# Two attention blocks on one core: v by the seven-product scheme used twice, in one row with output, k and q, and group statistics on ScalarE

## The chip, the cores and the metric

The kernel runs on one core of a Trainium2 chip. The metric is the device time of one execution in microseconds (us). In the text TensorE is PE in the profile (its weight loads PEld), VectorE is DVE, ScalarE is ACT, GpSimd is POOL, and SP is the engine that issues most DMAs.

## The reference, cut to what matters

Two attention blocks follow each other on x of shape (8, 512, 32, 32), all float32. Both compute the same thing up to the order of the weights:

```python
xn  = group_norm(x, 8 groups over channels and pixels) * gamma + beta      # (B, C=512, S=1024)
q, k, v = (W[i] @ xn + b[i] for i in range(3))                             # 512 x 512 each
p   = softmax(q_h^T k_h / 8) for each of 8 heads of 64 channels            # 1024 x 1024
out = concat_h(p_h v_h)
x   = x + Wp @ out + bp
```

The second block takes the first block's x.

## The kernel before

**Jobs.** A job is one image in one block; there are 16. They are ordered in groups of four: two images in the first block, then the same two in the second. A job has a *row* of projections and an *attention*. The row of job n computes v of job n, then the output projection (O) of job n - 1, then k and q of job n. The attention of job n follows.

**Seven products.** A product of two matrices, each cut in 2 x 2 blocks, is formed from seven block products instead of eight. The sums of weight blocks are kept in seven slots (`A11, S3, A12, A22, S1, S2, S4`); sums of the other operand's blocks are made by `combine` (into `tx`, `to` and in place). `v_phase` uses the scheme once: 7 products, each for two groups of tokens, each of four matmuls with 256 moving columns; that is 56 matmuls. Its blocks are put together in two PSUM bank groups, a result copied by ScalarE or added by VectorE into v. `deep_phases` uses the scheme twice for O, k and q: each of the seven outer products is again a chain of seven matmuls of 128 x 128 x 256, 49 in all for each. The inner sums of the other operand come from `inner_sums` (tile `deep`, for k and q) or `OutputSums` (tiles `os`, for O). Chains overlap in pairs: product j of chain c stands at place 7c + 2j. Each chain takes four banks of one half of PSUM; halves alternate from chain to chain. Its first results go to a tile `p` from the pool `epool` (6 buffers, shared with the attention's e tiles), and VectorE adds these up (`outer`).

**Attention.** 64 steps: eight groups (four pairs of heads, two halves of the query pixels) of eight blocks of keys. In step i TensorE forms the scores (`scores`, 8 matmul instructions), ScalarE takes their exponential (`e`), VectorE adds e to `acc` for the row sums, and two steps later TensorE multiplies with v into `po` (`values`). After each group `finish` adds the two halves of `po` into q; after every second group the row sums are inverted and q is normalised. Work for the next job is put between the steps as `chores`: statistics, normalisation, `combine`, inner sums, and the first weight fetches.

**What sets the order.** TensorE, ScalarE and VectorE run each in the order in which the program was written out. Python code writes it, with a clock of its own (`clock`, `advance`, `later`) that says when a thing is appended. No scheduler moves anything on these three engines. SP issues DMAs in the order written; weights come through a ring of 7 tiles (`fetch`, `used`). PSUM is two halves; `banks` closes one pool and opens the next, and a tile that lies where an older one was waits for that one's last reader.

**Factors of the weights.** The first time that a weight factor of O, k or q is used, `prepare` makes its inner sums on VectorE (4 additions of 128 x 128) and stores the result in DRAM; later fetches bring the finished 448 KB. For v the fetched block of 256 KB is used as it is.

**Statistics.** For every job except 0 and 1 VectorE reads x with eight `bn_stats` of 128 x 512, as `extra` work from the row's sixteenth chain on and, what is left over, in the first steps of attention. Job 1's statistics are made by ScalarE in attention 0: four passes that sum x and four that sum squares, with the sums read out by `accum_out`.

**Lines that the steps touch** (of the kernel before): v's matmuls L494, its copies L518 and additions L520; the matmuls of O, k and q L636; chain copies L438 and L442, results L646 to L657; additions of `p` L668 and of x L684 and L682; inner sums L423 to L429; `combine` L385 to L391; accumulations of e L893 and L895; in `finish` the reduction L925, the copy px L931 and the addition q<-po,px L932.

Of the kernel before, what the change touches and what calls it, by code (L numbers as in the profile page):

```python
# [9 lines left out]
F32 = mybir.dt.float32  # L10
# [9 lines left out]
P = 128  # L20
# [26 lines left out]
RING = 7  # L47
BLOCK = {1: (0, 0), 2: (0, 1), 4: (1, 1)}


# [22 lines left out]
def fast_path(  # L73
# [99 lines left out]
    def fetch():  # L173


        if not plan or len(held) == RING:
            return
        key = plan.popleft()
        n, which, o = key
        layer = jobs[n][1]  # L180
        w = ring.tile([P, NW, P], F32, tag="w", name=f"w_{which}_{n}_{o}")
        held[key] = w
        if (which, layer, o) in deep:
            nc.sync.dma_start(w, deep[which, layer, o])
        else:
            if o in BLOCK:
                src = raw_block(layer, which, *BLOCK[o])
            else:
                src = factors[which, layer][:, FACTOR[o]]
            nc.sync.dma_start(wide(w), src)  # L190
            if which != V:
                raw.add(key)
# [162 lines left out]
    def norm_steps(n):  # L355
# [5 lines left out]
        def factors():  # L361
            norm.factors(slice(0, NC))
            if n > 1:
                place()

        if n == 1:
            reads = [place] + [lambda cc=cc: norm.sums(cc) for cc in range(NC)]
            reads.append(norm.less_mean)
            reads += [lambda cc=cc: norm.squares(cc) for cc in range(NC)]
            reads.append(lambda: (norm.by_count(), norm.gather()))  # L370
            return reads, [norm.groups, factors] + [lambda cc=cc: norm.apply(cc) for cc in range(NC)]
# [202 lines left out]
    def deep_phases(n, extra, outs=None, early=()):  # L574
# [4 lines left out]
        dst = {}  # L579
        chains = [(which, o) for which in ((O, K, Q) if outs else (K, Q)) for o in OUTER]  # L580
        tiles = {}

        def job(which):
            return n - 1 if which == O else n

        def begin(c):
            which, o = chains[c]
            m = job(which)
            b, layer = jobs[m]
            if o == OUTER[0] and which != O:  # L590
                name = "k" if which == K else "q"
                dst[which] = acts.tile([P, NC, S], F32, tag=name, name=f"{name}_{n}")
                (kt if which == K else qt)[0] = dst[which]
            if c + 2 < len(chains):
                ahead, oo = chains[c + 2]
                prepare((job(ahead), ahead, oo))
            if which == O and c in (3, 4):
                soon.extend(outs.steps(c + 2))
            e = epool.tile([P, 2, HALF], F32, tag="e", name=f"p_{n}_{c}")
            tiles[which, o] = e  # L600
            s5 = small.tile([P, QT], F32, tag="s5", name=f"s5_{n}_{c}", bufs=3)
            half = (c + len(chains)) % 2
# [3 lines left out]
            if which == O:  # L606
                r = right(outs.src, to[0], o)
                sums = outs.at[c]
            else:
# [24 lines left out]

            def product(i, ps, start):
                nc.tensor.matmul(  # L636
                    ps, lhs[:, FACTOR[i], :], moving[i], start=start, stop=True,
                    skip_group_check=True,
                )

            def put(oo, ph, ps):
                to_ = e[:, oo, ph * QT : (ph + 1) * QT]
                b = bias(oo)
# [15 lines left out]
        def end(c):  # L659
# [6 lines left out]

            def add(to_, a, b):
                outer.append(lambda: nc.vector.tensor_add(to_, a, b))  # L668

            if which == O:  # L670
# [3 lines left out]
                def more(oh, sh, part, moved=False):  # L674
# [5 lines left out]
                    def go():  # L680
                        if moved:
                            nc.gpsimd.dma_start(to_, p(part), accum_op=ALU.add)  # L682
                        else:
                            nc.vector.tensor_add(to_, to_, p(part))  # L684
                        parts[oh, sh] -= 1
                        waiting[oh, sh] -= 1
# [19 lines left out]
                elif o == 6:  # L706
                    add(p(6), p(6), p(1))
                    more(0, 1, 6)
# [3 lines left out]
                elif o == 7:  # L712
                    add(p(7), p(7), p(6))
                    more(1, 0, 7)
# [5 lines left out]
                return  # L720
            d = dst[which]

            def quarter(oh, sh):
                return d[:, 2 * oh : 2 * oh + 2, sh * HALF : (sh + 1) * HALF]

            if o == 2:
                add(quarter(0, 0), p(1), p(2))
            elif o == 6:
                add(p(6), p(6), p(1))
            elif o == 5:  # L730
                add(quarter(0, 1), p(6), p(5))
            elif o == 7:
                add(p(7), p(7), p(6))
                add(quarter(1, 1), p(7), p(5))
            elif o == 3:
                add(quarter(0, 1), quarter(0, 1), p(3))
            elif o == 4:
                add(quarter(1, 0), p(7), p(4))

# [4 lines left out]
        def thunk(c, j):  # L744
            def go():
                if j == 0:
                    live[c] = begin(c)
                order = LAST_ORDER if c + 1 == len(chains) else ORDER
                live[c](order[j])
                if order[j] in (7, 3):  # L750
                    if soon:
# [7 lines left out]
                if j == 6:  # L759
                    end(c)  # L760
                    if c + 1 == len(chains):
                        while outer:
                            outer.popleft()()
                advance(0.43)

# [9 lines left out]
        ]  # L775
        return [thunk(c, j) for c, j in at]

# [80 lines left out]
    class Attention:  # L858
# [132 lines left out]

        def run(self, chores):

# [7 lines left out]
            for i in range(3, len(steps) + LEAD):  # L1001
                if i < len(steps):
                    self.scores(i)
                self.values(i - LEAD)
                g, kc = steps[i - LEAD]
# [27 lines left out]

    def out_sums(n, outs):

        def start():
# [3 lines left out]
        def part(i):  # L1042
            return lambda: combine(outs.src, to[0], i)

        c0, c1, c2, c3, c4 = (outs.steps(c) for c in range(5))
        steps = c0 + [start] + c3 + c1 + [part(1)] + c2 + [part(2)] + c4 + [part(3)]
        times = (0.1, 1.0, 2.5, 4.5, 5.5, 6.5, 7.5, 8.6, 14.0, 15.8, 16.5, 17.5, 19.2, 21.0)
# [20 lines left out]
    def extend_plan(n):  # L1068
        plan.extend((n, V, o) for o in ORDER)
        plan.extend((n - 1, O, o) for o in ORDER)  # L1070
        plan.extend((n, which, o) for which in (K, Q) for o in OUTER)
# [212 lines left out]
    for n in range(-1, len(jobs)):  # L1284
        last = n + 1 == len(jobs)
        outs = None
        if n >= 0:
# [11 lines left out]
            else:  # L1299
# [9 lines left out]
                if n == 0:  # L1309
                    for i, fn in zip((3, 3, 4, 5, 6, 8, 10, 11, 12, 13, 15), reads):  # L1310
                        put(i, fn)
                    at = (22, 30, 34, 35, 37, 38, 41, 44, 47, 50)
                for i, fn in zip(at, steps + sums(n + 1)):
                    put(i, fn)
                deep_first = deep_steps(n + 1)
                for at, fn in zip((52, 54, 57, 59), deep_first[4:]):
                    put(at, fn)
                put(61, lambda: (extend_plan(n + 1), [fetch() for _ in range(RING)]))
            assert max(chores, default=0) < NT * len(att.groups)
            att.run(chores)  # L1320
            banks(0, "one")
# [21 lines left out]
            if n + 2 < len(jobs):  # L1343
                reads, steps = norm_steps(n + 2)
                extra.extend((15, fn) for fn in reads)
        both = deep_phases(n + 1, extra, outs, deep_first[:4] if outs else ())
        both[0]()
# [260 lines left out]
```

## Time and profile before

| | |
|---|---|
| Time, median of 3 runs | 3204.76 us (3204.22 to 3205.25) |
| Profiled execution: span, first to last instruction | 3202.4 us |
| Outside the span | 2.4 us, by the median (the profiled execution has its span alone) |
| TensorE busy in the span | 3183.5 us (99%) |
| VectorE, ScalarE, GpSimd busy | 2773.9, 1914.3, 99.5 us |
| Row of job 3, row of job 6 | 90.14, 87.83 us |
| Attention of job 6 | 110.03 us |
| Granted TensorE clock | 0.999 |

A row of the timeline has the start in us from the span's start, its length in us, engine, line, operation, tiles (out<-in), shapes, and the count of instructions merged; in brackets stands how long the engine was idle before and what ended that. Instructions are pipelined: the length shown of one is longer than the distance to the next. A float32 matmul is two instructions in the trace.

### The profile page before, as it was taken

Reading aid. Unit: us, or ns where it says so; the run is one execution under the profiler, and the core shown is the slowest. Engines: PE = TensorE matmul, PEld = TensorE weight load, DVE = VectorE, ACT = ScalarE, POOL = GpSimd, SP = SyncE. Lnnn points to the kernel's source line nnn. Section 1 sums busy time; section 2 is a strip of 40 time slices with the busy share of each in tenths; the row PEclk is TensorE's granted clock in tenths of the full one; section 3 lists DMA queues with packets and bytes.
Section 4 is the critical chain, followed back from the end, with each engine's and each line's share of the span. In section 5 each row is a group of like instructions: output and inputs, shape, how many; then the busy total and the mean of one; then the engine's idle time right before and its main releaser. Section 6 shows DMA issues by size and latency. Waiting matters only on the chain.

```text
span 3202.4 us, 57786 instructions
## 1 busy us (share of the span) xinstructions
PE 3183.5 (99%) x22917; PEld 1862.2 (58%) x22917; DVE 2773.9 (87%) x3990; ACT 1914.3 (60%) x3063; POOL 99.5 (3%) x94
## 2 busy tenths in 40 slices
PE   9999999999999999999999999999999999999999
PEld 7366384663836648366483754837547375573744
DVE  8897999979889798897988889888898888978878
ACT  4746646466565665656656565565656656566564
POOL 0000000000000000000000000000000000000000
PEclk9999999999999999999999999999999999999999
DMA  8234172350713315034170421504316051150611
GB/s 291 74 105 123 49 216 67 95 166 22 213 25 90 89 28 158 22 105 130 31 211 16 117 69 37 149 16 137 101 44 194 16 138 48 49 136 16 174 37 42
DMA packets 156726, 307.80 MB, mean 96 GB/s; under 512 B 34088, under 2 KB 60576, under 8 KB 156192
## 3 DMA queue, kind: packets, MB, share of 16 engines
q1 hardware_dynamic: 139856, 272.05, 26.6%
q0 software_dynamic: 16592, 31.99, 6.1%
q8 instruction: 181, 2.97, 0.4%
q14 instruction: 97, 0.79, 0.1%
HBM read 225.13 MB, written 45.68 MB: 85 GB/s over the span
## 4 chain that ended last, share of the span: by engine, by line
PE 94%; DVE 5%; DMA 1%; issue 0%; ACT 0%; POOL 0%; DVEq 0%; SPq 0%; ACTq 0%; POOLq 0%
PE sc L878 27%; PE po L909 27%; PE zd L636 10%; PE vd L636 10%; PE z L494 6%; PE yd L636 5%; PE ud L636 4%; PE v L494 2%; PE y L494 2%; PE u L494 1%; DVE acc L895 1%; PE z_last L822 0%; DMA x<-p 0%; DMA w<-deep 0%; DVE w L156 0%
## 5 line engine op out<-in xcount | busy, mean ns | idle before, releaser
L883 ACT ACTIVATE e<-sc 128x1024 f32<-128x1024 f32 x1024 | 1045.0, 1024 | 563.6 <-PE sc L878 456.2
L878 PE MATMUL sc<-q,k 64*64 64x512 f32 x8192 | 1058.2, 589 | 0.0
L909 PE MATMUL po<-e,v 64*64 64x512 f32 x8192 | 1057.3, 589 | 0.0
L895 DVE TENSOR_TENSOR acc<-acc,e 128x1024 f32<-128x1024 f32 x768 | 936.2, 1219 | 58.7 <-ACT e L883 12.1
L909 PEld LDWEIGHTS po<-e,v 64*64 64x64 f32 x8192 | 313.2, 133 | 565.7 <-issue 552.9
L878 PEld LDWEIGHTS sc<-q,k 64*64 64x64 f32 x8192 | 311.6, 133 | 562.3 <-issue 544.2
L893 DVE TENSOR_TENSOR acc<-e,e 128x1024 f32<-128x1024 f32 x128 | 156.4, 1222 | 112.2 <-ACT e L883 112.1
L636 PE MATMUL zd<-deep,w 128*128 128x256 f32 x860 | 240.9, 379 | 1.1 <-DVE p L653 0.6
L636 PE MATMUL vd<-deep,w 128*128 128x256 f32 x804 | 224.4, 380 | 4.4 <-ACT yd L438 2.3
L636 PEld LDWEIGHTS zd<-deep,w 128*128 128x128 f32 x860 | 163.1, 190 | 24.7 <-DVE p L653 1.5
L636 PEld LDWEIGHTS vd<-deep,w 128*128 128x128 f32 x804 | 152.3, 190 | 27.2 <-ACT yd L438 2.7
L925 DVE TRANSPOSE_TENSOR_REDUCE r<-acc 128x32 f32<-128x1024 f32 x128 | 158.5, 1238 | 0.6
L682 POOL DMA_DIRECT2D x<-p x61 | 73.4, 1203 | 1974.0 <-ACT p L646 1408.5
L636 PE MATMUL vd<-os,w 128*128 128x256 f32 x420 | 118.2, 380 | 1.6 <-DVE p L655 1.5
L668 DVE TENSOR_TENSOR p<-p,p 128x1024 f32<-128x1024 f32 x94 | 114.2, 1215 | 0.0
L494 PE MATMUL z<-w,t 128*128 128x256 f32 x480 | 110.9, 379 | 0.0
L494 PE MATMUL z<-w,xn 128*128 128x256 f32 x480 | 110.1, 382 | 0.0
L518 ACT COPY v<-z 128x512 f32<-128x512 f32 x32 | 18.8, 586 | 148.7 <-PE z L494 148.7
L494 PEld LDWEIGHTS z<-w,xn 128*128 128x128 f32 x480 | 90.0, 190 | 23.8 <-issue 12.2
L442 ACT COPY ud<-zd 128x256 f32<-128x256 f32 x156 | 55.7, 357 | 76.5 <-PE zd L636 75.5
L653 DVE TENSOR_TENSOR p<-vd,s 128x256 f32<-128x256 f32 x63 | 26.7, 424 | 85.6 <-PE vd L636 85.6
L657 ACT COPY s<-vd 128x256 f32<-128x256 f32 x156 | 58.2, 373 | 70.1 <-PE vd L636 70.1
(242 smaller groups left out, 4193.8 us busy)
## 6 DMA issues: line engine op xcount, KB each, us to landing
w<-deep SPq DMA_DIRECT2D x287, 448.0 KB, 3.6
x<-p POOLq DMA_DIRECT2D x61, 512.0 KB, 6.5
rb<-rd SPq DMA_DIRECT2D x96, 256.0 KB, 4.1
w<-keep SPq DMA_DIRECT2D x84, 256.0 KB, 2.7
deep<-w SPq DMA_DIRECT2D x42, 448.0 KB, 3.3
w<-wqkv_dram SPq DMA_DIRECT2D x57, 256.0 KB, 2.8
x<-x_dram SPq DMA_DIRECT2D x28, 512.0 KB, 6.2
out_dram<-x SPq DMA_DIRECT2D x28, 512.0 KB, 6.0
```

The source lines that it names most:

```text
L442: nc.scalar.copy(u, z)
L494: nc.tensor.matmul(ps[:, ti * CH : (ti + 1) * CH], right(src, tx[0], o)[:, cc, t0 : t0 + P], w[:, cc, :], start=(start and ti == 0 and cc ...
L636: nc.tensor.matmul(ps, lhs[:, FACTOR[i], :], moving[i], start=start, stop=True, skip_group_check=True,)
L657: return chain(product, lambda ps: nc.scalar.copy(s5, ps), put, z, y, u, w)
L668: outer.append(lambda: nc.vector.tensor_add(to_, a, b))
L682: nc.gpsimd.dma_start(to_, p(part), accum_op=ALU.add)
L878: nc.tensor.matmul(sc[h * HD : (h + 1) * HD, j, :], k[r, hp, k0 : k0 + HD], q[r, hp, sh * HALF : (sh + 1) * HALF], start=True, stop=True,)
L883: nc.scalar.activation(e, sc, AF.Exp, scale=SCALE)
L893: nc.vector.tensor_add(acc[g], self.es[i - 1], e)
L895: nc.vector.tensor_add(acc[g], acc[g], e)
L909: nc.tensor.matmul(po[g][j * HD : (j + 1) * HD, h, :], v[r, kc, d0 : d0 + HD], e[r, j, :], start=(kc == 0), stop=(kc == NT - 1),)
L925: nc.vector.tensor_reduce(self.r[:, 0, m, :], self.acc.pop(g).rearrange("p j (b e) -> p (j b) e", e=RP), AX.X, ALU.add, apply_transpose=True,)
```

## The change

From job 3 on (`DEEP_V = 3`, the fourth job) v is computed in `deep_phases` too, as the first seven chains of one row with O, k and q:

- A v chain's product takes 128 tokens of the activations as the stationary operand and 128 columns of the weight factor as the moving one, twice (two halves of the 256 tokens): 98 matmuls of 128 x 128 x 128 for v of one job instead of 56 of 128 x 128 x 256. v's factors are now prepared and stored like the others; jobs 3 and 4 do this first for each block, 28 additions of 128 x 128 each, in the attention before.
- All four results of a v chain and its fifth product are copied out by ScalarE; VectorE then adds the fifth product (`add_five`, 128 x 512) and adds up whole tiles (`plus`, 128 x 1024): seven of each. For four of the seven chains (`PLACE`) the results go straight into v (for k and q likewise, in all jobs) and not into a `p` tile.
- `pump` and `next_work` decide by the writing clock what VectorE does after each product: the output sums with due times (`plan_sums`, `planned`), v's additions (`values`), the rest (`outer`, `extra`). `p_tile` keeps count of the `epool` tiles in use.
- The first two products of the row are written ahead of the attention's last `values` (`between`).
- Statistics of jobs 4 to 15 are made by ScalarE in the attention before, in steps 4 to 14; `bn_stats` for them goes.
- The chores of attention move: normalisation and `combine` to steps 20 to 41, all eight inner sums to steps 43 to 58 (before: four at 52 to 59, four in the row), v's seven fetches to step 46 (23 in attentions 2 and 3).

```diff
+DEEP_V = 3
+OUTER_V = (1, 6, 7, 2, 3, 5, 4)
...
-        if n == 1:
+        if n == 1 or n > DEEP_V:
             reads = [place] + [lambda cc=cc: norm.sums(cc) for cc in range(NC)]
...
+        with_v = n >= DEEP_V
+        kinds = ((V,) if with_v else ()) + ((O,) if outs else ()) + (K, Q)
+        chains = [(which, o) for which in kinds for o in (OUTER_V if which == V else OUTER)]
...
             def product(i, ps, start):
+                if which == V:
+                    for ti in range(2):
+                        tokens = slice(ti * P, (ti + 1) * P)
+                        nc.tensor.matmul(
+                            ps[:, tokens], moving[i][:, tokens], lhs[:, FACTOR[i], :],
+                            start=(start and ti == 0), stop=True, skip_group_check=True,
+                        )
+                    return
...
             def put(oo, ph, ps):
+                if which == V:
+                    nc.scalar.copy(
+                        e[:, 2 * ph : 2 * ph + 2, oo * P : (oo + 1) * P],
+                        ps.rearrange("p (t c) -> p t c", t=2),
+                    )
+                    return
...
+                values.append((0.62, add_five))
+                for to_, a in {
+                    6: ((6, 1),), 7: ((7, 6),), 2: ((2, 1),), 3: ((6, 3),), 5: ((6, 5), (5, 7)),
+                    4: ((7, 4),),
+                }.get(o, ()):
+                    plus(to_, a)
+                return
...
+                if with_v:
+                    if chains[c][0] == V:
+                        pump(c)
+                    elif order[j] in (7, 3):
+                        spend(0.38)
+                        pump(c)
...
+                if i - LEAD == len(steps) - 1 and between:
+                    between()
                 self.values(i - LEAD)
...
+                elif n >= DEEP_V:
+                    for i, fn in zip((3, 3, 4, 5, 6, 8, 9, 10, 11, 12, 14), reads):
+                        put(i, fn)
+                    at = (20, 27, 28, 30, 31, 33, 35, 37, 39, 41)
+                elif n + 1 == DEEP_V:
+                    at = (10, 19, 22, 24, 26, 28, 30, 32, 35, 38)
...
+                if n + 1 >= DEEP_V:
+                    for at, fn in zip((43, 45, 47, 49, 51, 53, 56, 58), deep_first):
+                        put(at, fn)
+                else:
+                    for at, fn in zip((52, 54, 57, 59), deep_first[4:]):
+                        put(at, fn)
...
+            if n + 1 >= DEEP_V and not last:
+                outs = OutputSums(n)
...
+                def between():
+                    banks(0, "one")
+                    both[0]()
+                    both[1]()
+
+                att.run(chores, between)
+                extra = ahead
+                plan_sums()
+                banks(1, "one")
```

## The prediction

> **What bounds the kernel now.** I read the page first, then the sums by stretch for one job, then the timelines of VectorE and TensorE where one job's attention hands over to the next row.
>
> ```profile
> span 3202.4 us, 57786 instructions
> PE 3183.5 (99%) x22917; PEld 1862.2 (58%) x22917; DVE 2773.9 (87%) x3990; ACT 1914.3 (60%) x3063; POOL 99.5 (3%) x94
> PE 94%; DVE 5%; DMA 1%; issue 0%; ACT 0%; POOL 0%; DVEq 0%; SPq 0%; ACTq 0%; POOLq 0%
> ```
>
> TensorE is busy all the time and carries the chain that ended last. A job is a row (v, output of the job before, k, q) and an attention; here are both for job 6.
>
> ```profile
> 1193.69:1281.52 87.83, 87.83 (x410) 77.00 (x407) 71.82 (x123) 46.60 (x116) 4.80 (x4) 1.00 0.56 150
> 1281.52:1391.54 110.03, 110.03 (x1025) 39.06 (x1025) 98.78 (x115) 73.12 (x76) 1.42 (x1) 1.00 0.08 21
> ```
>
> The columns are the stretch, its length, then PE, PEld, DVE, ACT and POOL busy. The row is pure TensorE pitch: 56 matmuls of v and 147 of the others, 203 x 0.4318 us = 87.66. From job 4 on every row takes 87.83, every attention 110.03. So anything that shortens TensorE's work pays in full, if VectorE, busy 98.78 of 110.03 us in attention, keeps up. Whether it does is seen at the handover:
>
> ```profile
> 1140.81 1.23 DVE L893 TENSOR_TENSOR acc<-e,e 128x1024 f32<-128x1024 f32 x1 [1.48 <-ACT e L883]
> ```
>
> ```profile
> 1187.34 2.55 DVE L895 TENSOR_TENSOR acc<-acc,e 128x1024 f32<-128x1024 f32 x2
> 1189.80 0.95 DVE L429 TENSOR_TENSOR deep<-t,deep 128x768 f32<-128x768 f32 x1
> 1190.67 5.21 DVE L895 TENSOR_TENSOR acc<-acc,e 128x1024 f32<-128x1024 f32 x4
> 1195.91 1.25 DVE L925 TRANSPOSE_TENSOR_REDUCE r<-acc 128x32 f32<-128x1024 f32 x1
> 1197.08 0.65 DVE L932 TENSOR_TENSOR q<-po,px 128x512 f32<-128x512 f32 x1
> ```
>
> ```profile
> 1216.40 1.22 DVE L391 TENSOR_TENSOR to<-q,to 128x1024 f32<-128x1024 f32 x1
> 1220.76 0.42 DVE L653 TENSOR_TENSOR p<-vd,s 128x256 f32<-128x256 f32 x1 [3.14 <-PE vd L636]
> ```
>
> VectorE last waits for work at 1140.81 (half way through the attention), and next at 1217.6. In between, 77 us, its queue is full (gaps of 0.10 between chained accumulations, one of 0.24). The add that frees the last attention bank (L932) ends at 1197.73, 4.04 after the row began at 1193.69. In this kernel nobody minds: the product that reuses that bank is the 13th matmul of v, at 1198.9.
>
> **TensorE's part.** A matmul of 256 columns is two instructions:
>
> ```profile
> 1009.76 3.62 PE L494 MATMUL z<-w,xn 128*128 128x256 f32 x16
> 1013.21 1.03 PE L494 MATMUL u<-w,xn 128*128 128x256 f32 x4
> ```
>
> 16 start in 3.45 us: 0.2158 each. The change replaces 56 x 2 instructions of 256 columns (24.18 us) by 49 products x 2 token halves x 2 = 196 of 128 columns, each with a weight load of its own. Columns alone give half of 0.2158, 0.108. The load has to fit as well, and the start of the kernel shows loads with almost nothing between them (matmuls of one column):
>
> ```profile
> 6.32 0.30 PEld L341 LDWEIGHTS pvar<-dev,blk 128*128 128x128 f32 x2 [0.65 <-DVE mr L337]
> 6.54 0.30 PEld L1130 LDWEIGHTS first_y<-blk 128*128 128x128 f32 x2
> ```
>
> Two loads start in 0.22 us, so 0.11 each, though each is shown 0.19 us long. That row is the nearest; I take 0.111. v is then 196 x 0.111 = 21.76: **2.42 us less per row**. With 0.108 the gain is 3.0. The far end is a pitch of the whole 0.190: 37.2 us, a loss of 13.1.
>
> The Trainium skill ("TensorE: Matmul & The Clock Gate", section "Back-to-back issue gap") speaks against the change: for streams of load and matmul it gives 81 ns at 128 columns where columns and floor alone give 55.8. An estimate by that ratio, 1.45, puts v at 31 us and would add 9 us to each of 13 rows beside what follows. No 128-column matmul is in this trace, but the loads at 0.11 are.
>
> **VectorE at the end of attention.** All eight inner sums now stand in attention; four of them (deep<-xn, 1.13 us from start to start) used to be issued in the row. In the built order they stand between accumulations, after the point at 1140.81. Two chained accumulations start 1.33 apart; with a sum between them, 1.14 + 1.13. Each sum thus adds 0.94 to 1.13, four of them 3.8 to 4.5; I take 4.0. The statistics that leave VectorE don't pay for this: three of the eight stood in attention, all before 1140.81, where VectorE idles anyway, and five at the row's end. So the add that frees the bank ends 8.04 us after the last attention matmul of the old layout, not 4.04.
>
> TensorE needs it sooner. In the built order two v products stand before the last group of attention matmuls and two behind it; then comes the second chain's first product, which waits for just this add in all 13 changed rows. TensorE is there 4 x 0.444 = 1.78 us after that same point. **Wait: 8.04 - 1.78 = 6.3 us**, bounds 5.0 (sums partly hidden) and 7.5. Everything of the row is queued behind it.
>
> A second queue limit lies behind the first. Up to the first output put VectorE had 3.14 us to spare. It gains 4.0 of lateness, six half-tile adds at 0.60 and six whole ones at 1.14 for v (10.4), loses four v puts (2.4) and defers two sums of 1.14 and four of 0.35 (3.7), while the put is due 2.4 earlier: 4.0 + 10.4 - 2.4 - 3.7 + 2.4 - 3.1 = 7.6 late. About 1.1 us pass from there to the product that needs the put, so 6.5. It is not added: while TensorE stands in the first wait, VectorE catches up on the second. But it says that lifting the first wait alone would buy little.
>
> **Rows 3 and 4.** The first use of each layer's v factors is prepared in attentions 2 and 3: 28 additions started every 0.205 us, 5.7 us, less about 0.8 for accumulations that they keep apart: 4.9 later, a wait of 11.2. Row 3 already lost 2.3 (90.14 against 87.83), which I leave.
>
> **ScalarE.** Eight statistics passes enter 12 attentions. Attention 0 already does this:
>
> ```profile
> 80.71:190.84 110.13, 110.13 (x1025) 38.96 (x1025) 100.06 (x122) 80.76 (x92) 2.06 (x1) 1.00 0.19 59
> ```
>
> It is 0.10 longer than the others. The change sets the four squares in four steps in a row, 2.03 us of ScalarE per step of 1.716, right behind a copy of 0.62: I take 0.3 per attention (0 to 0.6), 3.6 in all. In v each product gives ScalarE one copy, 0.357 to 0.373 against a product of 0.444: covered; at 0.475, the longest such read of a bank, it would cost 49 x 0.03 = 1.5 per row.
>
> **Edits at nothing.** v's weights grow from 256 to 448 KB; such a fetch lands in 3.6 us and seven are in flight, over 20 us ahead (3.6 us a factor if the ring ran dry). On SP's queue the seven fetches are issued at step 46 of attention instead of 61; 3.1 MB at the 200 GB/s that busy slices of the page show are 16 us, gone before the copy of the last row sums (4.1 us to land) is due at step 58; were it late, VectorE would be later by that much. POOL's additions into x keep their place. Two more whole adds are left over when the row ends, 2.3 us in front of attention's first accumulations; VectorE idles more than that before 1140.81. Jobs 0 to 2 move a few k and q adds and nothing else.
>
> **The sum.** Rows 5 to 15: 11 x (6.3 - 2.42) = 42.7. Rows 3 and 4: 2 x (11.2 - 2.42) = 17.6. Statistics 3.6. Together +63.9: the span goes from 3202.4 to 3266, and the median, which lies 2.4 above the span, from 3204.76 to **3268**.
>
> **Rivals.** (1) Faster: VectorE's queue gives way. The point that decides is the end of the bank's add: the wait must be under 2.42, so the add must end within 4.2 us of the last attention matmul, hardly later than now. For it: 11 us of idle VectorE in each attention and 4 us of statistics gone. Against it: that idle lies ahead of 1140.81, and the four sums need xn normalised and combined first, which comes after. With no wait at all the kernel takes 3204.8 - 13 x 2.42 + 3.6 = 3177; chance 0.09. (2) No change: the four sums vanish in gaps and only the earlier need stays, a wait of 4.04 - 1.78 = 2.26 against 2.42: 3206, chance 0.03. (3) Weight loads don't overlap at 128 columns: pitch 0.19, 13.1 lost per row beside the waits: 3204.8 + 63.9 + 13 x 15.5 = 3470; for it the shown length, against it the 0.11 above; chance 0.04.
>
> **How the numbers follow.** The forecast has 0.84. Its own range comes from the bounds: a steady wait of 5.0 gives 14 less, 7.5 gives 13 more, rows 3 and 4 up to 10 either way, the pitch 8 less, ScalarE's copies 20 more; with some room for both queue limits adding up, 3225 to 3300. That holds 0.80 in all, so it is the range. 0.2% is 6.4 us, about what a measurement of this kernel can tell from no change. Faster 0.09, same 0.03, slower 0.88.
>
> **What would show it.** Right: in the changed kernel TensorE waits for the add q<-po once in each of 13 rows, some 6 us in eleven and 11 in two; rows take about 91.7 and attentions 110.1 to 110.6; v's instructions start 0.111 apart; VectorE runs without a gap from mid-attention into the row. Wrong: rows of 85.4 without that wait, or v's instructions well over 0.111 apart, or the wait sitting at the output's puts instead, which would leave the time and move the cause.

## The result and the profile after

| | before | after |
|---|---|---|
| Time, median (lowest to highest) | 3205.01 us (3204.22 to 3206.52) | 3394.55 us (3391.34 to 3395.26) |
| Span of the profiled execution | 3202.4 us | 3393.5 us |
| Granted TensorE clock | 0.999 | 0.979 |
| Rows, attentions, summed over the kernel | 1403.1, 1760.5 us | 1558.7, 1792.1 us |

The ratio is 1.059 (1.0575 to 1.0605): 189.5 us slower, where 63 were forecast. The sums in the last line go from stage to stage by TensorE's first instruction: rows have grown by 155.6 us, attentions by 31.6, the last projection by 2.6 (the two profiled spans differ by 191.1). The page, in its first and fourth part:

```profile
span 3393.5 us, 60913 instructions
PE 3227.1 (95%) x24009; PEld 1908.1 (56%) x24009; DVE 2859.0 (84%) x4056; ACT 2161.5 (64%) x3762; POOL 89.1 (3%) x94
PE 5%; DMA 0%; DVE 0%; ACT 0%; issue 0%; DVEq 0%; ACTq 0%
```

TensorE fell from 99% to 95% busy. The chain breaks off after 5% this time and says nothing; the list of TensorE's waits has to be read instead (waiter, what ended the wait, us in total, times, longest):

```profile
PE vd L729 <- DVE q L1059: 80.4, 13, 7.7
PE vd L734 <- ACT yd L442: 46.0, 14, 4.6
PE sc L1005 <- ACT e L1010: 15.7, 18, 1.8
```

The first line is the forecast wait for the add that frees the last bank, once in each of 13 rows. The second and third were not forecast. Here is the handover into row 7, VectorE first, then TensorE, then stretches of that row and its attention (length; PE, PEld, DVE, ACT, POOL busy; granted clock; DMA share; GB/s):

```profile
1465.57 2.56 DVE L1022 TENSOR_TENSOR acc<-acc,e 128x1024 f32<-128x1024 f32 x2 [0.46 <-DVE acc L1022]
1468.16 1.25 DVE L1052 TRANSPOSE_TENSOR_REDUCE r<-acc 128x32 f32<-128x1024 f32 x1
1469.33 0.65 DVE L1059 TENSOR_TENSOR q<-po,px 128x512 f32<-128x512 f32 x1
```

```profile
1463.19 0.61 PE L729 MATMUL yd<-w,xn 128*128 128x128 f32 x4
1470.03 1.23 PE L729 MATMUL vd<-w,t 128*128 128x128 f32 x4 [6.24 <-DVE q L1059]
1471.05 1.06 PE L729 MATMUL vd<-w,deep 128*128 128x128 f32 x4
1477.46 0.61 PE L729 MATMUL zd<-w,deep 128*128 128x128 f32 x4
1477.90 0.61 PE L729 MATMUL vd<-w,deep 128*128 128x128 f32 x4
```

```profile
1470.00:1477.00 7.00, 6.97 (x40) 6.97 (x41) 6.77 (x17) 3.17 (x9) 0.00 (x0) 0.63 0.09 15
1462.64:1559.08 96.44, 87.59 (x487) 79.12 (x483) 73.47 (x121) 58.13 (x153) 4.80 (x4) 0.96 0.65 191
1559.08:1670.17 111.09, 109.97 (x1018) 38.35 (x1017) 100.25 (x115) 80.54 (x92) 0.56 (x1) 1.00 0.10 24
```

Three things to see. The wait is 6.24 us (6.3 were forecast). After it four instructions take 0.85 us, and only from about 1475 on 0.445: the granted clock is 0.63 in these 7 us. And the attention, which in these bounds lacks its last group of matmuls (1.02 us), is 111.09 long. The trace records from when to when a clock was granted. It shows 0.50 for 6.83 us (10.24 in row 3) at the start of every changed row, and for 3.41 or 6.83 us more in eleven of them, most some 49 us after the row begins. Half of their length, less the time in which TensorE was standing anyway, is 51 us.

The later wait is read one step further back, at what ScalarE itself waited for (ScalarE's waits), with the DMA's issue and TensorE's row in the same job:

```profile
ACT p L750 <- DMA x<-p: 59.2, 14, 5.5
```

```profile
1504.61 1.20 POOL L812 DMA_DIRECT2D x<-p  x1 [5.58 <-ACT yd L442]
```

```profile
1510.26 0.37 ACT L750 COPY p<-yd 128x256 f32<-128x256 f32 x1 [3.56 <-DMA x<-p]
1510.96 0.70 PE L734 MATMUL vd<-os,w 128*128 128x256 f32 x2 [2.61 <-ACT yd L442]
```

In the written order the p tile of the output's fifth chain is that of its second, whose addition into x is a DMA issued at 1504.61 and landed some 5.6 us later. ScalarE wants to write the tile before that.

In attention, two places. The four squares stand in four successive steps and push the exponential (and the next scores) 0.76 us back in all; and the first pass that applies the normalisation stands in front of an exponential while VectorE has not yet reached the offset:

```profile
1610.29 1.24 ACT L315 ACTIVATE xn<-x,off,mul 128x1024 f32<-128x1024 f32 x1 [1.93 <-DVE off L310]
```

```profile
1612.49 1.09 PE L1005 MATMUL sc<-q,k 64*64 64x512 f32 x8 [0.93 <-ACT e L1010]
```

Step by step against the attention before (starts of the scores), this one falls 0.76 us behind at the squares and 1.17 us more at this pass, and nothing elsewhere.

### The profile page after: what moved, and what is told of

It reads as the page before. It is cut to its first block, busy times and chain, and to the rows that moved or that the text cites. A ratio compares the mean times of both kernels' runs of the same rounds, so it can differ in the third digit from the quotient of the medians.

```text
span 3393.5 us, 60913 instructions
## 1 busy us (share of the span) xinstructions
PE 3227.1 (95%) x24009; PEld 1908.1 (56%) x24009; DVE 2859.0 (84%) x4056; ACT 2161.5 (64%) x3762; POOL 89.1 (3%) x94
## 5 line engine op out<-in xcount | busy, mean ns | idle before, releaser
L1005 PE MATMUL sc<-q,k 64*64 64x512 f32 x8192 | 1061.0, 591 | 18.0 <-ACT e L1010 15.7
L1020 DVE TENSOR_TENSOR acc<-e,e 128x1024 f32<-128x1024 f32 x128 | 156.3, 1221 | 74.7 <-ACT e L1010 74.7
L442 ACT COPY yd<-vd 128x256 f32<-128x256 f32 x209 | 75.0, 359 | 118.4 <-PE vd L729 106.4
L446 ACT COPY ud<-vd 128x256 f32<-128x256 f32 x209 | 74.6, 357 | 84.1 <-PE vd L734 70.7
L761 ACT COPY s<-zd 128x256 f32<-128x256 f32 x209 | 77.9, 373 | 78.7 <-PE zd L734 68.8
L729 PE MATMUL vd<-w,deep 128*128 128x128 f32 x780 | 123.1, 296 | 0.0
L729 PEld LDWEIGHTS vd<-w,deep 128*128 128x128 f32 x780 | 110.9, 212 | 10.5 <-ACT s L761 8.9
L761 ACT COPY s<-vd 128x256 f32<-128x256 f32 x195 | 72.6, 372 | 68.2 <-PE vd L734 64.5
L446 ACT COPY ud<-zd 128x256 f32<-128x256 f32 x195 | 69.6, 357 | 71.1 <-PE zd L734 68.3
L734 PE MATMUL zd<-os,w 128*128 128x256 f32 x352 | 105.0, 401 | 3.8 <-DVE p L757 3.1
```

The source lines that it names most:

```text
L442: nc.scalar.copy(y, z)
L446: nc.scalar.copy(u, z)
L729: nc.tensor.matmul(ps[:, tokens], moving[i][:, tokens], lhs[:, FACTOR[i], :], start=(start and ti == 0), stop=True, skip_group_check=True,)
L734: nc.tensor.matmul(ps, lhs[:, FACTOR[i], :], moving[i], start=start, stop=True, skip_group_check=True,)
L761: return chain(product, lambda ps: nc.scalar.copy(s5, ps), put, z, y, u, w)
L1005: nc.tensor.matmul(sc[h * HD : (h + 1) * HD, j, :], k[r, hp, k0 : k0 + HD], q[r, hp, sh * HALF : (sh + 1) * HALF], start=True, stop=True,)
```

## The experiments

Each is compared with the kernel before on the same chip (3204.3 to 3205.5 us); ratios are against it, with 95% intervals.

**Where the loss sits.** Undo v alone:

```diff
-DEEP_V = 3
+DEEP_V = 16
```

> v goes back to the seven-product scheme used once, with its own 56 matmuls, the statistics on VectorE and the inner sums in the row (DEEP_V = 16); only the new order of the additions into k and q stays. Theory (the 190 us come from v's chains, the order at the handover and the chores that moved with them): rows back at 87.8, attentions at 110.0, no granted clock of 0.5, time 3205, within 6 us. Rival (the k and q results that are added up in place, in longer chains, cost VectorE or the pool of p tiles something themselves): about 1 us per row, 3215 to 3225.

3205.23 us, ratio 1.0001 (0.9992 to 1.0011). The changed additions of k and q cost nothing; all of the loss comes with v's chains and what moved with them.

**The half clock.** Fill the wait:

```diff
+    if i == 2:
+        for _ in range(12):
+            nc.tensor.matmul(
+                idle_bank[0], env.blk, env.blk.unsqueeze(1).to_broadcast([P, 2, P]),
+                start=False, stop=True, skip_group_check=True,
+            )
     thunk()
```

> Everything of the change stays, the wait for the bank too; twelve idle matmuls (128 x 128 x 256, 12 x 0.432 = 5.2 us) stand on TensorE in front of the second v chain's first product and run while it would wait. Theory (the half clock follows from standing still): the clock record of 0.5 at the start of the 13 rows goes, v's instructions stay 0.111 apart, 13 x 3.4 = 44 us less: 3350. Rival (the half clock follows from the v matmuls or from something at the row's start): the record of 6.83 us at 0.5 stays and the time stays at 3394.

3362.82 us, 1.0497 (1.0480 to 1.0515): 31.7 less. Of 15 records of 6.83 us or more in rows one is left, and TensorE still waits for the same add (13.0 us beside the idle matmuls). So the half clock follows from standing still, not from v's matmuls. It gave 32 and not 44 because each record begins before the wait is over (1.7 us in job 7), where half a clock costs nothing. Shorter waits can do it too. In job 7 none follows the wait of 2.61 us shown above; in job 8 of the plain change, TensorE's wait and then a stretch with its granted clock (0.50):

```profile
1719.83 0.70 PE L734 MATMUL vd<-os,w 128*128 128x256 f32 x2 [2.71 <-ACT yd L442]
1720.90:1724.25 3.35, 3.35 (x10) 2.60 (x9) 2.08 (x4) 1.23 (x4) 0.00 (x0) 0.50 0.98 316
```

The Trainium skill ("TensorE: Matmul & The Clock Gate", section "Part 1: The HAM clock gate") states a rule: the clock is halved after an idle window of about 3.4 us, and the windows run free. The records agree in this: they show 0.50, last multiples of 3.41 us, begin on one grid of 3.413 us through the whole kernel, and stand at every wait of 6 us. They do not agree in the length of the idle time: 2.71 us in job 8 is less than such a window. There the measurement decides; what tells job 8 from job 7 is not shown.

**The bank.** At the end of attention, the add first:

```diff
-            if i > 2:
+            if 2 < i < self.late:
                 self.add(i)
...
             nc.vector.tensor_add(to_, p[:, 1, :], px)
+            if held_back:
+                for i in range(self.late, len(self.steps)):
+                    acc, e = self.acc, self.held[i]
+                    nc.vector.tensor_add(acc[g], acc[g], e)
+                row_sums()
```

> Everything of the change stays; at the end of each attention ahead of a changed row VectorE does the addition q<-po,px, which frees the last PSUM bank, ahead of the last four accumulations and the row sum instead of behind them (some 6 us earlier in its queue). Theory (TensorE waits 80.4 us for that addition, and the clock of 0.5 for 6.83 us at each row's start, 3.4 us lost, is a consequence of standing still for 6 us): the wait falls to at most 1 us per row and the half clock at the row's start goes, so 3394.6 - 70 - 44 = 3280, the waits in the output's part of the row unchanged. Rival (the prediction's second limit: VectorE is late for the first result of the output in any case): the row stands 6.5 us later on instead, 3365 or more. Rival 2 (the half clock belongs to the v matmuls of 128 columns, not to the wait): the wait goes and the clock record stays, 3325.

3360.56 us, 1.0489 (1.0468 to 1.0510). The wait for the bank is gone (6.0 us in 13), and TensorE stands at the output's first result instead:

```profile
PE zd L734 <- DVE p L757: 92.3, 17, 8.4
PE vd L729 <- DVE q L1067: 6.0, 13, 1.1
```

```profile
1693.12 1.22 PE L734 MATMUL zd<-os,w 128*128 128x256 f32 x2 [6.76 <-DVE p L757]
```

6.7 us, and the half clock behind it. The rival holds (3365 expected): the prediction's second limit, put there at 6.5. What was gained in sum is the wait for the DMA (46.0 us became 12.2), probably because TensorE now stands before that point long enough; that was not tested.

**The DMA in the output's part.** First all four additions on VectorE, then only the second chain's:

```diff
 def more(oh, sh, part, moved=False):
+    moved = moved and not with_v
```

> Everything of the change stays; in the 13 changed rows the four additions of p into x that GpSimd starts as DMAs (1.2 us to issue, 5 to 10 us to land) are done by VectorE instead, 1.22 us each. Theory (the 46 us that TensorE waits in the output's part of the row, once per row, come from a p tile that such a DMA still reads when ScalarE is to write it again; the second record of half clock in many rows follows from that wait): the wait goes, the second record goes too (1.7 us of time each in ten rows), 3394.6 - 46 - 17 = 3332, the wait for the bank unchanged. Rival (VectorE has no room for 4.9 us more per row in that part): p tiles come free as late as before or later, 3385 or more.

3369.36 us, 1.0513 (1.0496 to 1.0531). The wait is gone, but VectorE's extra work makes two others (18.3 us at the output's results, 21.4 us at attention's first scores, for q). 25 us gained where the next run gives 66: the rival holds in part.

```diff
-                    more(0, 0, 2, True)
+                    more(0, 0, 2, not with_v)
```

> The plain change, with one edit: of the four additions into x that GpSimd starts as DMAs, the one of the second output chain is done by VectorE (1.22 us). Theory (that DMA still reads the p tile that the fifth output chain is to write): the one wait per row in the output's part, 46 us in all, goes, and the second record of half clock of many rows with it (73 us at half speed less 13 first ones of 3.4 leave some 20 us): 3394.6 - 66 = 3329, up to 3345. Rival (another tile is as late, as where all four additions went to VectorE and 25 us came of it): 3365 or more.

3328.97 us, 1.0388 (1.0371 to 1.0405), 65.6 less, where the theory had 66. The wait <- ACT yd is 1.3 us, and all second records of half clock are gone (one in each of the 13 rows is left). One addition of 1.22 us, moved to VectorE, was worth 45 us of waiting and, reckoned as above, 22 of half clock (51 became 29).

**Attention.** The first pass one step later, then the statistics back on VectorE:

```diff
-at = (20, 27, 28, 30, 31, 33, 35, 37, 39, 41)
+at = (20, 27, 29, 30, 31, 33, 35, 37, 39, 41)
```

> Everything of the change stays; in attention the first ScalarE pass that applies the normalisation moves from step 28 to step 29, so VectorE has 1.7 us more for the scale and offset that this pass reads. Theory (1.17 of the 1.93 us that each attention has grown is ScalarE waiting for that offset, with the exponential of the next scores behind it; the other 0.76 are the four squares): attention shrinks by 1.0 to 1.2 us, 12 of them, 3394.6 - 13 = 3381. Rival (VectorE's queue is late at any such place, or the passes bunched at steps 29 to 31 cost the same): no change, 3391 to 3396.

3362.86 us, 1.0496 (1.0478 to 1.0513). Attention went from 111.09 to 110.03, 1.06 each, as expected (the kernel before has 109.01 in these bounds). The other 19 us are not in attention: the wait for the DMA fell to 36.6 us and the records of half clock from 26 to 19, their cost from 51 to 41 us.

```diff
-        if n == 1 or n > DEEP_V:
+        if n == 1:
```

> Everything of the change stays, but the statistics of jobs 4 to 15 are read by VectorE again (eight bn_stats of 0.6 us, in steps 3 to 10 of attention, where VectorE waits for work), and ScalarE's eight passes go. Theory (the four squares in four successive steps cost each attention 0.76 us): attention 0.76 us shorter, 12 of them, 9 us less: 3385; the 1.17 us of the wait for the offset stay. Rival (the bn_stats make VectorE later at the handover, or ScalarE's passes cost nothing): no change or slower, 3392 or more.

3375.06 us, 1.0526 (1.0509 to 1.0544). Attention went from 111.09 to 110.65, 0.44 and not 0.76, as the wait for the offset grew by 0.3. Most of the rest came from the row again (38.3 us of DMA wait, 47 of half clock).

**Do the terms add up?** All four costs that the prediction had missed taken away, the wait for the bank left and filled:

> The plain change with every cost taken away that the prediction had missed, and the one left that it had named: the wait for the bank stands as it is but is filled with twelve idle matmuls (no half clock), the second output chain's addition is done by VectorE (no wait for the DMA), statistics on VectorE and the first pass of the normalisation one step later (attention as before). Theory (the prediction's own terms hold and the rest of the excess is these four): 3204.8 - 13 x 2.42 + 80 for the bank + some 12 in attentions 2 and 3 and row 3 = 3265, 3255 to 3290. Rival (something unnamed is left): 3310 or more.

3299.01 us, 1.0294 (1.0277 to 1.0312), granted clock 0.998. The edits are those of the four runs with idle matmuls, with one addition, with the later pass and with the statistics on VectorE; together they give 95.5 us. The time lies 9 us above the expected range, and below the rival's. Of the 31 us that are left over the forecast of 3268, the trace puts some 19 in the rows and 11 in the attentions. Named are: v takes 22.3 us and not 21.76, since at a change between v's matmuls and those of attention, or the idle ones, an instruction takes 0.205 to 0.214 us instead of 0.112 (7 us in 13 rows); 12.6 us of waits at the output's results; attentions 2 and 3, which prepare v's factors, 2.8 and 3.5 us longer than before; and most others at 109.6, not 109.0 as before. The list does not close to the last microsecond.

**Is VectorE's lateness the cause?** Inner sums on GpSimd, alone and with two other edits:

```diff
-            inner_sums(part, direct)
+            inner_sums(part, direct, nc.gpsimd if n >= DEEP_V else nc.vector)
```

> Everything of the change stays; the eight inner sums of v, k and q in attention are done by GpSimd (idle there) instead of VectorE. Theory (VectorE's lateness at the handover is made of the queue since the middle of attention, four sums of the change and four old ones, 0.94 to 1.13 us each): VectorE is 7.5 to 9 us earlier, the wait of 6 us for the bank goes and the half clock at the row's start with it, and the second limit at the first result of the output is met as well: 3394.6 - 75 - 44 = 3275, the wait for the DMA in the output's part left. Rival (the two engines slow each other, or GpSimd's sums are too late for the row): accumulations longer than 1.22 us while GpSimd works, or a new wait of TensorE for deep; 3340 or more.

3457.03 us, 1.0785 (1.0767 to 1.0803). The rival holds; VectorE, then GpSimd:

```profile
1453.73 17.66 DVE L1022 TENSOR_TENSOR acc<-acc,e 128x1024 f32<-128x1024 f32 x6
```

```profile
1456.11 3.21 POOL L433 TENSOR_TENSOR deep<-xn,deep 128x1024 f32<-128x1024 f32 x1
```

Six accumulations take 17.66 us, 2.94 each against 1.3 elsewhere, about as long as GpSimd's sums beside them (2.67 to 3.34 us). The Trainium skill ("GPSIMD Engine Reference", section "1. Specifications") says that GpSimd shares its interfaces to SBUF with VectorE and that they contend when VectorE reads two operands from SBUF, as these additions do; the trace agrees, and gives the price.

> Three edits on the change: the inner sums on GpSimd, the addition that frees the last bank ahead of the last four accumulations, the first pass that applies the normalisation one step later. Theory: no wait of over 1 us is left at the handover and at the output's first result, no half clock at the row's start, attention 1.2 us shorter: 3394.6 - 80 - 44 - 14 = 3257 with the wait for the DMA in the output's part, 3195 if that goes as well, and then faster than the kernel before, as 13 x 2.4 us of TensorE's work are gone. Rival (GpSimd and VectorE slow each other): 3330 or more.

3444.77 us, 1.0744 (1.0726 to 1.0762): nearly the same loss. TensorE waits 73.5 us for exponentials in attention here and 86.3 us in the run before, where the plain change has 15.7.

Next, all of normalisation and the sums early, and the statistics on VectorE in the row's last chains (the core of the edit):

```diff
-                    at = (20, 27, 28, 30, 31, 33, 35, 37, 39, 41)
+                    at = (6, 10, 12, 14, 16, 18, 19, 20, 22, 24)
...
-                    for at, fn in zip((43, 45, 47, 49, 51, 53, 56, 58), deep_first):
+                    for at, fn in zip((43, 45, 47, 49, 51, 53, 56, 58) if n < DEEP_V else (26, 28, 30, 32, 34, 36, 38, 40), deep_first):
...
+                    ahead.extend((15, fn) for fn in reads)
```

> Everything of v's change stays, and all eight inner sums stay in attention on VectorE; but they move forward from steps 43 to 58 to steps 26 to 40, behind a normalisation moved forward too (ScalarE's passes at steps 12 to 18), which is possible because the statistics are read by VectorE again, in the last chains of the row, where it has idle time. Theory (VectorE's lateness is not the count of its operations but their place: 8.2 us of idle time in attention lie ahead of the sums and can't be used): VectorE catches up before the attention ends, the wait of 6 us for the bank and the half clock at the row's start go (75 + 44), the 6.7 us behind them too, attentions return to 110.0 (23): 3394.6 - 142 = 3252 with the wait for the DMA in the output's part, 3190 if it goes. Rival (VectorE has too much work in the 196 us of a job for any place: its lateness returns at the handover): a wait of 3 us or more per row, 3300 or more.

3374.69 us, 1.0529 (1.0512 to 1.0547): 20 less, not 140. The wait for the bank halved (41.4 us, 2.4 in most rows), so place matters, and hardly any wait at the output's first result stands behind it:

```profile
PE zd L734 <- DVE p L757: 9.1, 11, 3.1
```

The DMA wait stayed (42.7 us), and in seven rows the statistics waited for a new x, with the next chain's results behind them in VectorE's queue and TensorE behind those (28.3 us):

```profile
1537.82 0.69 DVE L238 BATCH_NORM_STATS2 stats<-x 128x6 f32<-128x512 f32 x1 [6.37 <-DMA x<-x_dram]
```

> The kernel with the early sums, and in addition the addition that frees the last bank ahead of the last four accumulations of attention. Theory: where the early sums leave some lateness, this takes the rest of the wait for the bank; at most 0.5 us of it per row, and no record of half clock at the row's start; 0 to 40 us below the kernel with the early sums alone. Rival (as in the run with this edit on the plain change): the wait moves to the output's first result, no gain.

3401.83 us, 1.0615 (1.0597 to 1.0632): slower by 27. The wait moves, as the rival has it, and grows: 5.2 us are left at the bank, and 92.4 stand at the output's first result.

> The kernel with both edits, and in addition one of the four additions by DMA, that of the second output chain, done by VectorE (1.22 us). Theory (ScalarE waits for the p tile that this DMA still reads): the wait for a DMA in the output's part of the row goes, with VectorE 1.2 us busier where it has idle time; up to 46 + 17 us below the kernel without it, and then below the kernel before: rows of 85.4 and attentions of 110.0 would give 3204.8 - 13 x 2.42 = 3173. Rival (VectorE late there, or another DMA's tile is next): half of it or less.

3381.24 us, 1.0544 (1.0527 to 1.0562). The DMA wait went, but the second limit was there again, 6.7 us in most rows, and here VectorE was not late at the handover:

```profile
1456.53 0.69 DVE L1069 TENSOR_TENSOR q<-po,px 128x512 f32<-128x512 f32 x1 [3.56 <-ACT px L1068]
...
1487.81 0.42 DVE L757 TENSOR_TENSOR p<-zd,s 128x256 f32<-128x256 f32 x1
```

It had idled for 3.56 us, then worked without a gap for 31.3 us up to the output's first result. TensorE has 24.3 us of work there. Of the 31.3, four accumulations (5.0 us) and a reduction (1.25) are attention's: "bank first" puts them behind the add, and VectorE idles ahead of it while they could have begun. With the early sums alone, where they stand ahead of the add, this wait is 9.1 us in all, though TensorE comes to it later there, by the 2.4 us at the bank. So here the edit itself makes much of the second limit. The rest of the 31.3, some 25 us of the last steps of the row sums, output sums and v's additions, is about as long as TensorE's work. How the 6.7 us of the plain change with the bank first divide into lateness from attention and work of the row, no run shows.

**Place or amount?** v's last additions deferred, on the kernel with the bank first; then all four edits:

```diff
-                    values.append((1.14, go))
+                    if o in (5, 4):
+                        outer.append(go)
+                    else:
+                        values.append((1.14, go))
```

> The plain change with the bank's addition ahead of the last four accumulations, and in addition v's last three additions (1.14 us each) behind the output's first results. Theory (the 6.7 us wait at the output's first result is the sum of VectorE's work queued ahead of it): that wait falls by 3.4 to about 3.3 us per row, 13 x 3.4 = 44 us, and the half clock of 6.83 us behind it shortens in part: 3300 to 3320. Rival (the wait is lateness brought along from attention or hangs on something else): it stays at 6.7, 3360.

3348.30 us, 1.0446 (1.0430 to 1.0462). The wait moved by 0.5 only: the writing clock put output sums of later chains where the additions had been. Of the 12 us gained, 8 are the wait for the DMA (12.2 us became 3.8).

> Four edits on the change: statistics on VectorE at the row's end (later than before in rows that load a new x) with all of normalisation and inner sums early; the addition that frees the bank ahead of the last two accumulations; the second output chain's addition into x on VectorE; and v's last three additions (1.14 us each) behind the output's first results instead of ahead of them. Theory (between the handover and the output's first result VectorE has 31.3 us of work queued against some 24 us of TensorE; it is that sum which makes the second limit, at any lateness; the early sums take 5 us of accumulations out of it, the deferred additions 3.4): no wait over 1 us at the handover nor at the output's first result, no half clock in most rows, rows of 86 to 88, attentions of 110.0: 3180 to 3215. Rival (VectorE's total is too much: the deferred additions come back as waits for p tiles in the output's part): 3250 or more.

3349.51 us, 1.0451 (1.0437 to 1.0465). Here two waits at the output's results, 3.7 and 2.1 us, are left in each row. The clock of the program takes VectorE to be 10 us behind at the row's start; its first addition for v starts 13.6 us after it. So that constant was raised, to 15.0 with all edits and to 17.0 on the kernel with only the bank first:

```diff
-AHEAD, TAIL = 0.8, 10.0
+AHEAD, TAIL = 0.8, 15.0
```

> The kernel with four edits, and two constants more: the writing clock's guess of how far VectorE is behind when a row begins (TAIL) is 15.0 us instead of 10.0, so some 5 us of VectorE's additions are written behind the output's first results instead of ahead of them; and the normalisation's passes begin two steps later (the offset is late by up to 3.5 us in every second attention otherwise). Theory (the second limit is the place of VectorE's work within the row): the waits of 3.65 and 2.05 us for the output's results, once each per row, fall under 1 us, the half clock goes with them, 47 + 27 + 35 us, and 15 in the attentions: 3349.5 - 124 = 3226, 3215 to 3260. Rival (VectorE's work only comes back later in the row, as waits for k's or q's results or p tiles): 3300 or more.

> The plain change with the bank's addition ahead of the last four accumulations, and with that guess (TAIL) at 17.0 us instead of 10.0; nothing else. Theory: the wait of 6.7 us for the output's first result falls to 1.5 us or less and the 6.83 us of half clock behind it go: 3360.6 - 13 x (5.2 + 3.4) = 3249, up to 3290 if some of the wait returns at the next results. Rival (the wait is set by lateness from attention or by the sum of the row's work, wherever it is placed): 3340 or more.

3281.10 us, 1.0236 (1.0222 to 1.0250), the lowest of all runs that keep v's change, and 3363.90 us, 1.0494 (1.0478 to 1.0510). With the early sums the 3.7 us went, and 68 us of time: 47 in the rows, and 23 in the attentions, where the passes stand later; one wait of 2.6 us per row is left and eleven records of 3.41 us. The rival's 3300 was not reached, nor the theory's 3260. Without them the place gained nothing: the wait for the first result fell to 15.2 us in all, and 74.7 us came back at p tiles (ScalarE waiting for a DMA again, 87.1 us). So the place of VectorE's work matters, but it can't be chosen freely: what is put off keeps v's p tiles busy (read from the written order, not tested by itself). No version here beats the kernel before; rows of 85.4 us were not reached, and what would be needed stays open.

## Why the prediction was wrong

- **Direction and the wait for the bank: right.** TensorE waits for q<-po,px in 13 rows: 80.4 us where 11 x 6.3 + 2 x 11.2 = 91.7 were forecast. The steady wait is some 5.9 us; rows 3 and 4 have 7.7 and not 11.2. Attentions 2 and 3, where v's factors are prepared, grew by 2.8 and 4.4 us instead, which the sum did not have; whether the one is the price of the other was not tested.
- **Pitch: nearly right.** Within v, four instructions start 0.446 us apart, 0.1115 each (forecast 0.111, not the 0.19 of the shown length, nor the 31 us of the back-to-back rule that was weighed). The changes between v's matmuls and attention's were missed (three instructions of 0.205 to 0.214 us per row): the gain is 2.0 us per row, not 2.42.
- **The step that failed first: the price of a wait.** "Everything of the row is queued behind it" counted the wait as its own length. Standing for 6 us also halves the clock behind it: 35 us in the records of 6.83 us and more, 51 in all; filling the wait gave 31.7 back. The profile of before shows 0.5 only at its edges; its longest wait of TensorE is 2.3 us.
- **The second: "POOL's additions into x keep their place", an edit at nothing.** Their place in the queue was kept, the life of their p tiles was not: v takes tiles from the same pool of six. 46 us of waiting, 66 us in all by the run that moved one of them.
- **The third: "I take 0.3 per attention (0 to 0.6)".** The squares cost 0.76, outside the bounds. The scale and offset, moved to one step ahead of the pass that reads them, were not costed: 1.17.
- **The second limit: right in size, its cause in part open.** 6.5 forecast, 6.7 measured once the first wait was lifted, and lifting the first alone did buy little (34 us, the wait for the DMA). That 6.7 came again where VectorE had idled before is no proof against the sum's term for lateness, 4.0: there the edit had put accumulations of attention into the row. That the two figures agree so closely may be luck in part.
- **Costed at nothing and rightly so:** the k and q additions (1.0001), v's copies by ScalarE and the larger fetches; no wait for either stands among those listed.
- **The range.** Its own terms upwards, 13, 10 and 20 us on 3268, come to 3311, not 3300; the three prices above lie outside them all the same.

By the trace the three failed prices are 51 us of half clock, 46 of waiting for the DMA and 28 in the attentions (31.6 where 3.6 were forecast), about as much as the 126 us over the forecast; the smaller terms have either sign. 95.5 of the 126 were lifted by four edits on these prices together; that much is shown. How the 95.5 divide is not additive: alone the edits gave 31.7, 65.6, 31.7 and 19.5 us, 148.5 in sum, as each also shifted the others' waits and the records of half clock.

## What to carry to other kernels

Price a wait of TensorE with the clock behind it, and ask of every tile pool that gets a new user whose last reader is a slow DMA. A wait that is lifted shows the next one: before believing in a gain, add up the other engine's work between two handovers and compare it with TensorE's, since a queue that is too full there can keep the loss wherever it is moved. An operation put ahead in a queue also holds back what stands behind it while it waits itself. Two operations one step apart on two engines need the lateness of the first engine's queue between them, not the length of the operation.

## What had not been expected of the hardware

- A halved clock after waits as short as 2.5 us (job 11 of the plain change), in some rows and not in others. An edit in attention can change the time of rows: 19 us in the run that moved one pass, some 10 of it in half clock.
- VectorE's accumulations take 2.94 us and not 1.3 while GpSimd adds tensors of 128x1024 or 128x768 beside them.
- Matmul instructions of 128 columns keep 0.1115 us with a weight load each. Where they meet attention's matmuls, one instruction takes 0.1 us longer (three times per row); where they meet the output's 256 columns, none does (0.112).
